# A two-layer graph network on one core: row statistics of both norms from group sums and squared deviations on ScalarE

## The chip, the cores and the metric

The kernel runs on one core of a Trainium2 chip. The metric is the time of one execution on the device in microseconds. A core has five engines with an instruction queue each: TensorE (PE: matrix products, with its weight loads listed apart as PEld), VectorE (DVE), ScalarE (ACT), GpSimd (POOL) and SyncE (SP), which in this kernel issues the transfers (DMA). An engine works through its queue in order; semaphores make it wait for others. So an instruction that waits holds everything behind it in its own queue.

## The reference

128 graphs with 128 nodes of 256 features each go through two layers. Each layer normalises every row, takes the positive part, applies a graph layer and adds the result to its input.

```python
def _layernorm(x, axis=-1, eps=1e-5):
    m = jnp.mean(x, axis=axis, keepdims=True)
    v = jnp.var(x, axis=axis, keepdims=True)
    return (x - m) / jnp.sqrt(v + eps)
...
    h = jnp.maximum(_layernorm(x, axis=-1), 0.0)
    x = x + _L0_gnn_ref(h, adj, L0_gnn_weight, L0_gnn_bias)
    h = jnp.maximum(_layernorm(x, axis=-1), 0.0)
    x = x + _L1_gnn_ref(h, adj, L1_gnn_fc_w, ..., L1_gnn_fp_b)
    return x
```

The first graph layer is `adj @ (h @ weight) + bias`. The second is attention with 8 heads over the graph: logits from one query and one key number per node and head, a mask from the adjacency, a leaky rectifier, a softmax, the weighted sum, a projection back to 256 features, `+ fp_b + h`, and a sigmoid. All is float32.

## The kernel before

**Groups and stages.** The 128 graphs are worked in 32 groups of four (`GB = 4`). A tile of a group has the 128 nodes on the partitions and the four graphs side by side: `xg` is 128 x (4 x 256). A group passes through these stages, and several groups are in work at once, each at another stage:

- `begin` loads x and the adjacency. `n1_stats` takes mean and variance of each row, `n1_apply` (L330) makes h on ScalarE with `Relu(rstd * x + nb)`, where `nb = -mean * rstd`. `first_a` and `first_b` are the products of the first layer (L378, L394); the addition at L401 makes `x1`.
- `n2_stats` and `n2_apply` are the same for `x1`, and give `h2`. `move_h2` (L437) and `turn_h2_blocks` (L441) turn h2 by 16 transfers and a 32 x 32 block transpose; `make_qk` (L464), `turn_qk` (L478 to L484) and `load_k` (L489) make the attention's query and key numbers.
- `masked` (L509, L517, VectorE), `leaky` (L530, ScalarE), `head_max` (L538, VectorE), `exps` (L546, ScalarE, which also sums) and `normal` (L554 on VectorE, L555 on GpSimd) make the attention of one graph each; `move` (L566) and `turn` (L574) turn it.
- Four units a group (`aggregate` L596, `take` L613 to L622, `multiply` L641, `combine` L657 to L676) are the weighted sum and the projection. They use seven products in place of eight, with sums and differences f2 to f6 of the aggregates: `take` copies an aggregate on ScalarE (f0 L613, f3 L615, f1 L621) or works on VectorE (f4 L617, f6 L618), and GpSimd makes f5 (L619) and f2 (L622). A unit's products run one unit after its aggregates.
- `residual_a` (L680), `residual_b`, `sigmoid`, `finish` (L695), `store`.

**Row statistics.** `stats` works on half a group: for each of two graphs a `bn_stats` (L296) over 256 elements and a `bn_aggr` (L297) that gives mean and variance, all on VectorE. `rdev` adds epsilon on VectorE (L308) and raises to the power -0.5 on GpSimd (L312); `shift` forms nb on VectorE (L319). In the loop `rdev_both` and `shift_both` do this together for the second norm of one group and the first norm of the next.

**Order.** All queues follow an order written by hand. A group of the loop has 44 slots; in each slot one step of TensorE's own list is put out (`ORDER`: four aggregates and seven products, four times over), and then the entries of `PLAN` for that slot, in their order in the list. An entry is (slot, which group or "u" for a unit, function, arguments); group 2 means the group two ahead of the current one. The first group has a list of its own, `FIRST_PLAN`, with most of its attention still made by other entries. Ahead of the loop the first groups' early stages are written out one by one; there `scale(..., root=True)` takes a square root on ScalarE (L306) in place of the power.

In the loop before the change, per group: both `n1_stats` at slot 28 (for the group four ahead), `n2_stats` at slots 37 and 40 (three ahead) each behind its `first_b`, `rdev_both` at slot 41, `take` of f1 and f2 at slot 42, `residual_a` at slot 43. In the next group's pass the same norms are then those of "group 2": slot 0 has a `take`, two `masked` and a `leaky`, slot 2 `shift_both`, slot 3 a `take`, the two `n2_apply` and `move_h2`, slots 4 and 5 further attention steps, slot 6 the first half of a `combine`, slot 18 `turn_h2_blocks`, slot 24 `make_qk`, slot 25 `n1_apply`.

Of the kernel before, what the change touches and what calls it, by code (L numbers as in the profile page):

```python
# [9 lines left out]
FP = mybir.dt.float32  # L10
AF = mybir.ActivationFunctionType
ALU = mybir.AluOpType
AX = mybir.AxisListType
PSUM = bass.MemoryType.PSUM

P = 128
D = 256
# [3 lines left out]
GB = 4  # L21
# [3 lines left out]
EPS = 1e-5  # L25
# [3 lines left out]
def gnn_then_gat_kernel(  # L29
# [16 lines left out]
    nc = tc.nc  # L46
    NG = x.shape[0] // GB

    const = ctx.enter_context(tc.tile_pool(name="const", bufs=1))
# [5 lines left out]
    nc.vector.memset(power, -0.5)  # L55
    eps = const.tile([P, 1], FP, name="eps")
    nc.vector.memset(eps, EPS)

    gp = ctx.enter_context(tc.tile_pool(name="group", bufs=2))
    at = ctx.enter_context(tc.tile_pool(name="attention", bufs=2))  # L60
    small = ctx.enter_context(tc.tile_pool(name="small", bufs=3))
# [228 lines left out]
    def stats(s, key, src, b0):  # L290

        if b0 == 0:
            s[key] = small.tile([P, GB, 2], FP, name="mv", tag="mv")
        st = small.tile([P, 2, 6], FP, name="st", tag="st")
        for b in range(2):
            nc.vector.bn_stats(st[:, b, :], src[:, b0 + b, :])  # L296
            nc.vector.bn_aggr(s[key][:, b0 + b, :], st[:, b, :])  # L297

    def rdev(*norms, root=False):

        n = len(norms)
        rstd = small.tile([P, n, GB], FP, name="rstd", tag="rstd")
        for i, (s, key) in enumerate(norms):
            s[key, "by"] = rstd[:, i]
            if root:
                nc.scalar.activation(rstd[:, i], s[key][:, :, 1], AF.Sqrt, bias=eps)  # L306
            else:
                nc.vector.tensor_scalar(rstd[:, i], s[key][:, :, 1], EPS, None, ALU.add)  # L308
        if root:
            nc.vector.reciprocal(rstd, rstd)  # L310
        else:
            nc.gpsimd.tensor_tensor(rstd, rstd, power[:, 0:n], ALU.pow)  # L312

    def shift(*norms):

        for s, key in norms:
            nb = small.tile([P, GB], FP, name="nb", tag="nb")
            rstd = s[key, "by"]
            nc.vector.scalar_tensor_tensor(  # L319
                nb, s[key][:, :, 0], -1.0, rstd, ALU.mult, ALU.mult  # L320
            )
            s[key, "by"] = (rstd, nb)

    def scale(*norms, root=False):
        rdev(*norms, root=root)
        shift(*norms)
# [10 lines left out]

    def n1_stats(s, half):
        stats(s, "n1", s["xg"], 2 * half)

    def n1_apply(s, half):
        if half == 0:
            s["h"] = gp.tile([P, GB, D], FP, name="h", tag="h", bufs=1)
        for b in range(2 * half, 2 * half + 2):
            apply(s, "n1", b, s["h"][:, b], s["xg"][:, b])
# [69 lines left out]
    def rdev_both(s):  # L415
        rdev(*norms_of(s))

    def shift_both(s):
        shift(*norms_of(s))
# [279 lines left out]
    def store(s, b0, nb):  # L699
# [9 lines left out]
    PLAN = [  # L709
        (0, "u", take, 0, 0, 0),  # L710
        (0, 1, masked, 0),
        (0, 1, masked, 1),
        (0, 1, leaky, 0),
        (2, 2, shift_both),
        (3, "u", take, 0, 1, 1),
        (3, 2, n2_apply, 0),
        (3, 2, n2_apply, 1),
        (3, 2, move_h2),
# [41 lines left out]
        (28, 1, move, 0, range(8, 16)),  # L760
        (28, 1, normal, 3),
        (28, 3, turn_blocks),
        (28, 4, n1_stats, 0),
        (28, 4, n1_stats, 1),
        (28, -1, sigmoid, 0, GB),
        (29, -1, finish, 0, GB),
        (29, 3, add_b0),
# [11 lines left out]
        (35, 3, first_a, 1),  # L779
        (36, "u", take, 3, 1, 1),  # L780
        (37, 3, first_b, 0),
        (37, 3, n2_stats, 0),
        (37, 3, make_mask),
        (39, "u", take, 3, 1, 0),
        (40, 3, first_b, 1),
        (40, 3, n2_stats, 1),
        (41, 3, rdev_both),
        (42, "u", take, 3, 0, 1),
        (43, 0, residual_a, 1),
    ]  # L790
# [21 lines left out]
        (17, "u", take, 1, 1, 0),  # L812
        (17, 1, leaky, 0),
        (18, 0, turn_by_products, 3),
        (18, 3, n1_stats, 0),
        (18, 3, n1_stats, 1),
        (20, "u", take, 1, 0, 1),
        (20, 1, masked, 1),
        (20, 2, first_a, 0),
# [6 lines left out]
        (23, 2, first_b, 0),  # L826
        (23, 2, first_b, 1),
        (24, 4, begin),
        (24, 2, n2_stats, 0),
        (24, 2, n2_stats, 1),  # L830
        (24, 2, rdev_both),
        (25, "u", take, 2, 1, 1),
        (25, 1, head_max, 1),
        (25, 1, normal, 0),
        (25, 2, shift_both),
        (26, 2, n2_apply, 0),
# [24 lines left out]
        (34, 3, turn_blocks),  # L861
        (36, "u", take, 3, 1, 1),
        (36, 0, setup_wqk_order),
        (36, 4, n1_stats, 0),
        (36, 4, n1_stats, 1),
        (36, 1, head_max, 3),
        (36, 1, normal, 2),
        (37, 3, first_a, 0),
# [2 lines left out]
        (38, 1, turn, 0),  # L871
        (39, "u", take, 3, 1, 0),
        (39, 3, first_b, 0),
        (39, 3, n2_stats, 0),
        (39, 1, turn, 1),
        (39, 1, normal, 3),
        (40, 1, move, 1),
        (41, 3, first_b, 1),
        (41, 3, n2_stats, 1),
        (41, 3, rdev_both),  # L880
        (42, "u", take, 3, 0, 1),
        (42, 3, make_mask),
        (43, 0, residual_a, 1),
# [80 lines left out]
    n2_stats(s1, 1)  # L964
    normal(s0, 0)
    rdev((s1, "n2"), (s2, "n1"))
    setup_weights(3, 0, True)
    setup_weights(3, 1, True)
# [3 lines left out]
    setup_weights(5, 1, True)  # L972
    normal(s0, 1)
    shift((s1, "n2"), (s2, "n1"))
    setup_weights(6, 0, True)
    setup_weights(6, 1, True)
# [22 lines left out]
    for g in range(NG):  # L999
# [4 lines left out]
        for slot in range(4 * len(ORDER)):  # L1004
            n, i = divmod(slot, len(ORDER))
# [58 lines left out]
```

## Time and profile before

| | |
|---|---|
| median of three runs | 1537.14 us (1533.25, 1537.14, 1537.39) |
| the profiled execution | 1530.25 us, of which 1528.5 us are its span |
| mean granted TensorE clock | 0.997 |
| transfers | 139.18 MB, the 16 DMA engines busy 40% |

The page of the profile gives the busy time of each engine, then the instructions grouped by line (busy time in all, mean duration in ns, idle time of the engine just ahead of them and what ended it). The rows of the statistics on it are these:

```profile
L296 DVE BATCH_NORM_STATS2 st<-x 128x6 f32<-128x256 f32 x128 | 52.5, 410 | 2.0
L312 POOL TENSOR_TENSOR rstd<-rstd,power 128x8 f32<-128x8 f32 (+1 forms) x31 | 50.5, 1629 | 48.0 <-DVE rstd L308 48.0
L296 DVE BATCH_NORM_STATS2 st<-xg 128x6 f32<-128x256 f32 x128 | 50.3, 393 | 3.7 <-DMA xg<-in_x_dram 3.7
L297 DVE BATCH_NORM_AGGREGATE mv<-st 128x2 f32<-128x6 f32 x256 | 46.6, 182 | 8.8
```

The means are durations; instructions of one engine overlap a little, so the pitch from start to start is smaller, and it is the pitch that fills a queue. A timeline line gives start and duration in us, engine, line, operation, tiles, the count, and in square brackets how long the engine had been idle and what released it. A line of the waits gives who waited for whom, then the total in us, how often, and the longest. Busy time by stretch shows the same picture in all groups of the loop; three of them are, with the columns stretch, its length, and busy time (and instructions) of PE, PEld, DVE, ACT and POOL, then TensorE's clock and the transfers:

```profile
562.00:608.00 46.00, 45.87 (x314) 37.34 (x313) 41.43 (x75) 34.84 (x124) 30.03 (x22) 1.00 0.44 97
608.00:653.00 45.00, 44.39 (x300) 35.59 (x299) 39.82 (x67) 33.12 (x117) 28.32 (x22) 1.00 0.43 93
653.00:698.00 45.00, 44.87 (x306) 36.36 (x306) 40.45 (x71) 33.84 (x120) 29.06 (x22) 1.00 0.44 98
```

### The profile page before, as it was taken

The page shows a single profiled execution, that of the slowest core. Times are in us where ns is not written, and L with a number is a line of the kernel's source. Part 1 is how long each engine was busy: PE and PEld are TensorE (multiplying, and loading weights), DVE is VectorE, ACT ScalarE, POOL GpSimd, SP SyncE. Part 2 cuts the span into 40 slices and gives each one's busy share as a digit, 9 for nine tenths or more (in the row PEclk, how much of TensorE's full clock was granted, in tenths as well). Part 3 has the DMA queues.
Part 4 walks back from the last instruction along what each step waited for, and adds up shares of the span by engine and source line. Part 5 has one row for each costly group of instructions (what it writes and reads, how often), then busy time and mean ns, then how long its engine had stood idle before and what let it go on. Part 6 is the DMA issues. An engine that isn't in the chain of part 4 may idle for free.

```text
span 1528.5 us, 30616 instructions
## 1 busy us (share of the span) xinstructions
PE 1481.2 (97%) x9969; PEld 1195.8 (78%) x9969; DVE 1312.9 (86%) x2275; ACT 1101.8 (72%) x3836; POOL 954.4 (62%) x698
## 2 busy tenths in 40 slices
PE   7788999999999999999999999999999999999998
PEld 6577888877788888788887887888778888878776
DVE  5888988888988888998888898888898888898763
ACT  4888677787677788677778776678766778876651
POOL 5556566665566766566766556666556676656563
PEclk9999999999999999999999999999999999999999
DMA  6123344444444444434444434444443444433320
GB/s 188 30 49 79 81 104 107 87 100 96 94 87 105 94 100 94 96 83 104 106 87 98 96 91 92 107 87 99 95 98 84 105 93 101 95 76 81 73 70 28
DMA packets 253736, 139.18 MB, mean 91 GB/s; under 512 B 169972, under 2 KB 221576, under 8 KB 253320
## 3 DMA queue, kind: packets, MB, share of 16 engines
q1 hardware_dynamic: 253576, 137.23, 40.0%
q8 instruction: 78, 1.28, 0.4%
q14 instruction: 82, 0.67, 0.2%
HBM read 39.60 MB, written 17.30 MB: 37 GB/s over the span
## 4 chain that ended last, share of the span: by engine, by line
ACT 32%; DVE 30%; SPq 11%; PE 9%; issue 6%; DMA 6%; POOL 4%; DVEq 0%; ACTq 0%; POOLq 0%
ACT attn L546 13%; ACT attn L530 11%; SPq L566 8%; DVE attn L517 7%; PE acc L641 5%; DVE attn L509 5%; ACT h L330 4%; DVE st L296 3%; DMA attnB<-attn 3%; DVE attnT L574 3%; PE g_ps L596 3%; SPq L437 2%; POOL attn L555 2%; DVE f L617 2%; DVE x L401 2%
## 5 line engine op out<-in xcount | busy, mean ns | idle before, releaser
L641 PEld LDWEIGHTS acc<-wts,f 128*128 128x128 f32 x7168 | 886.8, 192 | 249.3 <-issue 179.5
L641 PE MATMUL acc<-wts,f 128*128 128x128 f32 x7168 | 894.4, 275 | 5.5 <-DVE z L657 5.0
L596 PE MATMUL g_ps<-attnT,h 128*128 128x512 f32 x1024 | 526.5, 597 | 0.0
L546 ACT ACTIVATE attn<-attn,nmax 128x128 f32<-128x128 f32 x1024 | 397.7, 399 | 0.9 <-DVE nmax L538 0.9
L619 POOL TENSOR_TENSOR f<-f,f 128x512 f32<-128x512 f32 x128 | 163.4, 1277 | 341.5 <-DVE f L617 341.0
L530 ACT ACTIVATE attn<-attn,q 128x128 f32<-128x128 f32 x1024 | 313.3, 393 | 34.9 <-DMA attnB<-attn 19.2
L555 POOL TENSOR_TENSOR attn<-attn,total 128x1024 f32<-128x1024 f32 x128 | 246.2, 1923 | 101.6 <-DVE total L554 87.7
L621 ACT COPY f<-g_ps 128x512 f32<-128x512 f32 x128 | 73.9, 577 | 260.0 <-PE g_ps L596 260.0
L622 POOL TENSOR_TENSOR f<-f,f 128x512 f32<-128x512 f32 x128 | 208.8, 1632 | 9.6 <-ACT f L621 6.9
L546 ACT ACTIVATION_READ_ACCUMULATOR attn<-attn,nmax 128x1 f32 x1024 | 202.5, 198 | 0.0
L517 DVE TENSOR_TENSOR attn<-attn,mask 128x1024 f32<-128x1024 f32 x128 | 190.3, 1487 | 4.5
L538 DVE TENSOR_REDUCE nmax<-attn 128x8 f32<-128x1024 f32 x128 | 153.9, 1202 | 18.8 <-ACT attn L530 18.6
L596 PEld LDWEIGHTS g_ps<-attnT,h 128*128 128x128 f32 x1024 | 155.7, 192 | 8.0 <-issue 7.1
L509 DVE STREAM_TRANSPOSE attn<-kq 128x1024 f32<-128x1024 f32 x128 | 157.0, 1226 | 5.5 <-DMA kq<-k_mem 5.4
L574 DVE STREAM_TRANSPOSE attnT<-attnB 128x1024 f32<-128x1024 f32 x124 | 148.5, 1216 | 8.6 <-DMA attnB<-attn 5.9
L617 DVE TENSOR_TENSOR f<-g_ps,f 128x512 f32<-128x512 f32 x128 | 87.0, 680 | 48.0 <-issue 26.3
L394 PE MATMUL x_ps<-w_sb,ahT 128*128 128x256 f32 x512 | 121.3, 381 | 1.4 <-ACT ahT L385 1.4
L685 POOL TENSOR_TENSOR z<-z,h 128x256 f32<-128x256 f32 x128 | 90.7, 731 | 39.9 <-DVE z L657 39.9
L613 ACT COPY f<-g_ps 128x512 f32<-128x512 f32 x128 | 74.5, 582 | 41.6 <-PE g_ps L596 41.6
L394 PEld LDWEIGHTS x_ps<-w_sb,ahT 128*128 128x128 f32 x512 | 93.1, 191 | 12.4 <-ACT ahT L385 2.2
L695 DVE SCALAR_TENSOR_TENSOR z<-z,x 128x1024 f32<-128x1024 f32 (+1 forms) x33 | 89.2, 2703 | 7.9 <-ACT z L691 7.9
L618 DVE TENSOR_TENSOR f<-f,g_ps 128x512 f32<-128x512 f32 x128 | 86.4, 675 | 0.0
(100 smaller groups left out, 1286.1 us busy)
## 6 DMA issues: line engine op xcount, KB each, us to landing
attnB<-attn SPq DMA_DIRECT2D x992, 64.0 KB, 2.0
xg<-in_x_dram SPq DMA_DIRECT2D x32, 512.0 KB, 4.1
out_dram<-z SPq DMA_DIRECT2D x31, 512.0 KB, 3.1
h2B<-h SPq DMA_DIRECT2D x464, 32.0 KB, 1.9
ag<-in_adj_dram SPq DMA_DIRECT2D x32, 256.0 KB, 4.6
agB<-in_adj_dram SPq DMA_DIRECT2D x116, 64.0 KB, 4.4
fcw<-in_L_gnn_fc_w_dram SPq DMA_DIRECT2D x2, 1024.0 KB, 6.9
fpw<-in_L_gnn_fp_w_dram SPq DMA_DIRECT2D x1, 2048.0 KB, 14.1
```

The costliest lines, as they stand in the source:

```text
L394: nc.tensor.matmul(op[:, bb, :], lhsT=s["ahT"][:, 2 * b2 + bb, c, :], rhs=w0_sb[:, c, :], start=(c == 0), stop=(c == NC - 1),)
L509: nc.vector.transpose(s["v", b], s["kq"][:, :, b].unsqueeze(3).to_broadcast([P, NB, H, Q]),)
L517: nc.vector.tensor_tensor(a, a, s["mask"][:, b, :] .rearrange("p (j c) -> p j c", c=Q) .unsqueeze(2) .to_broadcast([P, NB, H, Q]), ALU.add,)
L530: nc.scalar.activation(a[:, :, h, :], a[:, :, h, :], AF.Prelu, bias=s["q"][:, b, h : h + 1], alpha=0.01,)
L538: nc.vector.tensor_reduce(nmax, a.rearrange("p j h c -> p h j c"), AX.XY, ALU.max, negate=True)
L546: nc.scalar.activation(a[:, :, h, :], a[:, :, h, :], AF.Exp, bias=s["nmax", b][:, h : h + 1], accum_out=s["total", b][:, h : h + 1],)
L555: nc.gpsimd.tensor_tensor(a, a, total.unsqueeze(1).unsqueeze(3).to_broadcast([P, NB, H, Q]), ALU.mult)
L574: nc.vector.transpose(aT.rearrange("p h (i r) -> p i h r", r=Q), s["ab", b // 2][:, :, b % 2])
L596: nc.tensor.matmul(u["g", b, c], lhsT=s["h2"][:, 2 * pair + b].rearrange("p j c q -> p (j c q)")[:, ts(c, P)], rhs=s["aT", 2 * pair + b][: ...
L619: nc.gpsimd.tensor_tensor(new(5), f[4], f[0], ALU.subtract)
L622: nc.gpsimd.tensor_tensor(new(2), f[1], f[5], ALU.subtract)
L641: nc.tensor.matmul(acc[:, slot, :], lhsT=u["f"][m][:, h, :], rhs=wt[m][:, half * HU + h, :], start=(half == 0 and h == 0 and m in FIRST), ...
```

## The change

Two new functions stand beside `stats`. `sums` takes one negated sum per row over all graphs given (four for n1, two for n2) with a single `tensor_reduce` on VectorE. `squares` runs one `Square` activation per graph on ScalarE, of `256 * x - sum`, whose accumulated output is 256 cubed times the variance; what it writes itself goes to a tile that nobody reads. `rdev` multiplies by the inverse of that factor in the instruction that adds epsilon, and `shift` takes the sum, divided by 256, in place of the mean.

```diff
+    def sums(s, key, src, b0, nb):
+        if b0 == 0:
+            s[key, "sum"] = small.tile([P, GB], FP, name="nsum", tag="nsum", bufs=4)
+            s[key, "sq"] = small.tile([P, GB], FP, name="sq", tag="sq", bufs=4)
+        nc.vector.tensor_reduce(
+            s[key, "sum"][:, b0 : b0 + nb], src[:, b0 : b0 + nb], AX.X, ALU.add, negate=True
+        )
+
+    def squares(s, key, src, b0, nb):
+        for b in range(b0, b0 + nb):
+            nc.scalar.activation(
+                squared, src[:, b], AF.Square, bias=s[key, "sum"][:, b : b + 1], scale=float(D),
+                accum_out=s[key, "sq"][:, b : b + 1],
+            )
...
-                nc.vector.tensor_scalar(rstd[:, i], s[key][:, :, 1], EPS, None, ALU.add)
+                if (key, "sq") in s:
+                    var, by = s[key, "sq"], float(D) ** -3
+                else:
+                    var, by = s[key][:, :, 1], 1.0
+                nc.vector.tensor_scalar(rstd[:, i], var, by, EPS, ALU.mult, ALU.add)
...
     PLAN = [
         (0, "u", take, 0, 0, 0),
         (0, 1, masked, 0),
+        (0, 2, rdev_both),
         (0, 1, masked, 1),
         (0, 1, leaky, 0),
-        (2, 2, shift_both),
         (3, "u", take, 0, 1, 1),
+        (3, 2, shift_both),
         (3, 2, n2_apply, 0),
...
-        (28, 4, n1_stats, 0),
-        (28, 4, n1_stats, 1),
+        (28, 4, n1_sums),
...
         (37, 3, first_b, 0),
-        (37, 3, n2_stats, 0),
+        (37, 3, n2_sums, 0),
+        (37, 4, n1_squares),
+        (37, 3, n2_squares, 0),
         (37, 3, make_mask),
         (39, "u", take, 3, 1, 0),
         (40, 3, first_b, 1),
-        (40, 3, n2_stats, 1),
-        (41, 3, rdev_both),
+        (40, 3, n2_sums, 1),
+        (40, 3, n2_squares, 1),
         (42, "u", take, 3, 0, 1),
```

`FIRST_PLAN` is changed in the same way: the n1 sums at slots 18 and 36, their squares at 20 and 39; for the group two ahead the n2 sums at slot 24, the squares and `rdev_both` at slot 25 (behind a `take` and a `head_max`); for the one three ahead the n2 sums and squares at slots 39 and 41, with `rdev_both` left to slot 0 of the next group. The statistics written out ahead of the loop still use `stats`.

More of the change, by code (lines that the diff above doesn't have):

```diff
@@ L57, in gnn_then_gat_kernel @@
     nc.vector.memset(eps, EPS)
+    squared = const.tile([P, D], FP, name="squared")
     gp = ctx.enter_context(tc.tile_pool(name="group", bufs=2))
@@ L318, in shift @@
             rstd = s[key, "by"]
-            nc.vector.scalar_tensor_tensor(
-                nb, s[key][:, :, 0], -1.0, rstd, ALU.mult, ALU.mult
-            )
+            if (key, "sum") in s:
+                mean, by = s[key, "sum"], 1.0 / D
+            else:
+                mean, by = s[key][:, :, 0], -1.0
+            nc.vector.scalar_tensor_tensor(nb, mean, by, rstd, ALU.mult, ALU.mult)
             s[key, "by"] = (rstd, nb)
@@ L339, in n1_stats, with n1_sums, n1_squares, n2_sums @@
         stats(s, "n1", s["xg"], 2 * half)
+    def n1_sums(s):
+        sums(s, "n1", s["xg"], 0, GB)
+    def n1_squares(s):
+        squares(s, "n1", s["xg"], 0, GB)
+    def n2_sums(s, half):
+        sums(s, "n2", s["x1"], 2 * half, 2)
+    def n2_squares(s, half):
+        squares(s, "n2", s["x1"], 2 * half, 2)
     def n1_apply(s, half):
@@ L814, in gnn_then_gat_kernel @@
         (18, 0, turn_by_products, 3),
-        (18, 3, n1_stats, 0),
-        (18, 3, n1_stats, 1),
+        (18, 3, n1_sums),
+        (20, 3, n1_squares),
         (20, "u", take, 1, 0, 1),
@@ L828, in gnn_then_gat_kernel @@
         (24, 4, begin),
-        (24, 2, n2_stats, 0),
-        (24, 2, n2_stats, 1),
-        (24, 2, rdev_both),
+        (24, 2, n2_sums, 0),
+        (24, 2, n2_sums, 1),
+        (25, 2, n2_squares, 0),
+        (25, 2, n2_squares, 1),
         (25, "u", take, 2, 1, 1),
         (25, 1, head_max, 1),
+        (25, 2, rdev_both),
         (25, 1, normal, 0),
@@ L863, in gnn_then_gat_kernel @@
         (36, 0, setup_wqk_order),
-        (36, 4, n1_stats, 0),
-        (36, 4, n1_stats, 1),
+        (36, 4, n1_sums),
         (36, 1, head_max, 3),
@@ L873, in gnn_then_gat_kernel @@
         (39, 3, first_b, 0),
-        (39, 3, n2_stats, 0),
+        (39, 3, n2_sums, 0),
+        (39, 4, n1_squares),
+        (39, 3, n2_squares, 0),
         (39, 1, turn, 1),
@@ L878, in gnn_then_gat_kernel @@
         (41, 3, first_b, 1),
-        (41, 3, n2_stats, 1),
-        (41, 3, rdev_both),
+        (41, 3, n2_sums, 1),
+        (41, 3, n2_squares, 1),
         (42, "u", take, 3, 0, 1),
```

## The prediction

> **What bounds the kernel now.** I read the page's first two parts, the waits, and then the timelines of all engines over one ordinary group of four graphs (606 to 655 us).
>
> ```profile
> span 1528.5 us, 30616 instructions
> PE 1481.2 (97%) x9969; PEld 1195.8 (78%) x9969; DVE 1312.9 (86%) x2275; ACT 1101.8 (72%) x3836; POOL 954.4 (62%) x698
> PE qk_ps L464 <- DVE h2T L441: 8.0, 19, 2.8
> PE acc L641 <- DVE z L657: 5.0, 6, 2.7
> ```
>
> TensorE is 97% busy, and where it waits inside the loop, it waits for VectorE: for h2T (L441) or for a combined accumulator (L657). The L464 instructions of the loop start at 147.6 us for the first and at 1417.1 for the last of its 29 times, 28 periods apart: with 0.4 us off, since the last start is the last of its own 16, 45.3 us a group. What would TensorE need unhindered? From start to start in its timeline a product of L641 (8 matmuls) takes 0.89 us, an aggregation of L596 0.86; a group has 28 and 16 of them, 25.0 + 13.8, and L378 1.79, L394 twice 1.73, L464 0.59, L478 0.11 make 44.75. So **the whole prize in the loop is 28 x 0.55 = 15 us**, however much VectorE work goes.
>
> The 0.55 consists of the hold before L464 in every group (0.20 is shown as idle; by starts, with modelled ends left aside, the 16 matmuls ahead begin at 643.60 and fill 1.78, to 645.38, so it is 0.35) and of a hold at L641 in some:
>
> ```profile
> 633.84 2.02 PE L641 MATMUL acc<-wts,f 128*128 128x128 f32 x16 [0.42 <-DVE z L657]
> 645.75 0.67 PE L464 MATMUL qk_ps<-h2T,wqk 128*32 128x128 f32 x16 [0.20 <-DVE h2T L441]
> ```
>
> Both have the same cause. VectorE's timeline shows no idle time between the turn at 615.84 and the head maxima at 646.46: a queue of 30 us, with the statistics of x1 in its first third. ScalarE is the second half of the circle: it starts at the first normalisation (629.26), works without a break to 659 us, and the f3 copies of that stretch release the turned k, the transfers behind it and so the next 615.84. So time saved in VectorE ahead of 629.08 (nb, L319) shortens the circle, and nothing else does.
>
> **The change part by part.** From the page's groups of instructions:
>
> ```profile
> L538 DVE TENSOR_REDUCE nmax<-attn 128x8 f32<-128x1024 f32 x128 | 153.9, 1202 | 18.8 <-ACT attn L530 18.6
> L330 ACT ACTIVATE h<-x,nb,rstd 128x256 f32<-128x256 f32 x128 | 66.4, 590 | 23.3 <-DVE nb L319 23.3
> ```
>
> and, from the timelines of ScalarE, VectorE and GpSimd over that group:
>
> ```profile
> 622.08 0.59 ACT L621 COPY f<-g_ps 128x512 f32<-128x512 f32 x1 [8.21 <-PE g_ps L596]
> 618.14 0.65 DVE L401 TENSOR_TENSOR x<-x_ps,xg 128x512 f32<-128x512 f32 x1
> 618.82 0.43 DVE L296 BATCH_NORM_STATS2 st<-x 128x6 f32<-128x256 f32 x1
> ...
> 621.09 0.68 DVE L401 TENSOR_TENSOR x<-x_ps,xg 128x512 f32<-128x512 f32 x1
> ...
> 623.34 1.65 POOL L312 TENSOR_TENSOR rstd<-rstd,power 128x8 f32<-128x8 f32 x1 [1.39 <-DVE rstd L308]
> 624.95 1.89 POOL L622 TENSOR_TENSOR f<-f,f 128x512 f32<-128x512 f32 x1
> 626.79 1.27 POOL L680 TENSOR_TENSOR h<-h,fpb_j 128x512 f32<-128x512 f32 x1
> 629.08 0.22 DVE L319 SCALAR_TENSOR_TENSOR nb<-mv,rstd 128x4 f32<-128x4 f32 x2
> ```
>
> *Input sums (n1), slot 28.* Removed: four pairs of L296 and L297, 0.53 us a pair from start to start, 2.1 us. Added: one reduction of 128x1024, the size of L538, 1.2 us. Saved 0.9 us, but off the path: the turn at 615.84 waits for a DMA (0.64 us idle), so VectorE only idles longer there. Worth 0.
>
> *x1 sums (n2), slots 37 and 40.* Removed twice two pairs, 1.1 us each (618.82 to 619.91). Added twice a reduction of 128x512; the trace has none over whole rows, so between half of L538 (0.60) and all of it (1.20); I take 0.65, since L538's time runs with its elements. Saved 0.45 each, 0.9 on the path (between 0 and 1).
>
> Here a rule speaks against the change. The Trainium skill, "VectorE: DVE Perf Modes", section Rules for kernel authors, calls `tensor_reduce` the slowest operation of this engine and says to restructure around it. Taken as it stands, no step to more reductions should gain. But L538 makes 1024 elements in 1.20 us and the eight bn instructions need 2.1 for the same, so the rows decide: 0.9 gained where the rule would put 0 or less.
>
> *Squares on ScalarE.* Eight a group, 128x256. Four of L330 start to end take 2.08 us, a pitch of 0.50; reading out the accumulator adds 0.09 (exps of L546 follow each other at 0.385, leaky units of the same size at 0.29). So 0.59 each, 4.7 us a group, 139 us for the 236 of them (n1 of 29 groups, n2 of 30); upper bound 0.80, if each waits for the full 0.20 us of the accumulator's row. The skill, "ScalarE: Activation LUTs", sections What ACT_TABLE_LOAD costs and Rules for kernel authors, would give 0.09 less (one pointer operand in place of two), and it leaves multiplications to VectorE. By that rule n2 alone would need products (half of L517's 1.23 us, twice) and two more reductions there, 2.5 us for 0.9 saved: 1.6 us a group lost on the path, 45 us in all. But the rows show VectorE without a gap here and ScalarE with one, so the engine that is slower by the element is the cheaper: I keep 0.59 and the idle time. What hides them: ScalarE is idle before 622.08 for 8.21 us. The four n1 squares run there from 613.9 to 616.3, and the first n2 pair at 619.5 to 620.7. Cover is enough even at 0.80. Only the second n2 pair is exposed: it waits for the second sum. Should Square need another table set, the one load of the trace (1283 ns) would come twice a group; the trace shows Prelu, Exp, Tanh, Relu and copies under one set, and I give the other 3 in 100.
>
> *rdev moved from slot 41 to behind the first mask, shift from slot 2 to 3.* Neither issues a DMA; SP's transfers of h2 (L437) wait for the h behind nb and move with it. VectorE doesn't wait for the squares at once: it has a mask to do first (2.4 us). But GpSimd gets the power (L312) behind L622 and L680 instead of ahead of them, and L622 waits for an f1 copy that on ScalarE now stands behind the second pair of squares. So there is a **new wait**: nb for the power. Queued behind nb on VectorE are the head maximum, two masks, the combination and h2T; all of the circle. The f1 copy itself, at 623.8 for 622.7, holds nobody: its product starts at 626.2, that of f2 (L622) at 631.5.
>
> The two ways to nb, from the second L401. It starts at 620.6 instead of 621.09 (0.45 saved before it) and ends at 621.25.
> - Through VectorE: sum 0.65, mask 2.4, rdev 0.2, mask 2.4, and up to 1.0 because an addition of L517 takes 2.26 instead of 1.23 us beside L680 (now at 626.89, and again likely): 626.9 to 627.9.
> - Through ScalarE and GpSimd: sum 0.7, two squares 1.25, copy 0.6, L622 1.3 to 1.9, L680 1.25, power 1.65, hand-over 0.1: 628.1 to 628.7; with squares at 0.80 and all collisions up to 629.2.
>
> The second ends last. So nb comes at 628.1 to 629.2, I take 628.5, **0.6 us earlier** than 629.08. The first mask needs kq, whose last transfer is issued about 619.6 and lands in 1.7 us, 621.3; it would start at 621.95, so this is covered, by 0.6. 0.6 is more than the 0.35 before L464 and enough for most of the holds at L641. What is late next is TensorE itself, at 44.75. I take 44.85 to 44.9, since single holds (1.3 us at 917 us) have other causes: **28 x 0.43 = 12 us saved**.
>
> *The first two groups lose.* In group 0 the reductions and squares stand on the way to the first turned h: ScalarE ends its exps at 91.45 and squares four times (2.4 us, with the last read-out to 94.0), so rdev comes at 94.0 instead of 92.42: 1.6 us, and TensorE's hold of 3.06 us at 96.97 grows by it. At the start of group 1 the power stands behind f1's copy, L622, the mask (L355) and L680 as well: sums of the same rows put nb at 129.7 instead of 127.83, 1.9 us, and the hold of 2.83 us before L464 grows. Together **3.5 us lost**. The statistics written out ahead of the loop stay as they are.
>
> Sum: -12 + 3.5 = -8.5 us. The profiled execution took 1530.25 us (1528.5 of span and 1.75 around it), so 1521.75, a factor of 0.9944. The median of the runs shown is 1537.14, 7 us above that execution; the factor gives **1528.6 us**.
>
> **Rivals.**
> 1. *No net gain (22 in 100).* The power ends at the late end, 629.1: nb stands where it was, the loop keeps 45.3, the 3.5 us remain: 1540.6. For it: the chain's many members. Against: it needs the upper value of each.
> 2. *Slower: nb waits for the power (22 in 100).* The place is slot 3, the point from which it decides is a power that ends after 629.0. TensorE has no slack to VectorE (holds of 0.35 already), so every 0.1 us later costs 28 x 0.1 = 2.8 us. At 0.5 us late, 14 + 3.5 = 17.5: 1554.7. For it: L622 took 2.25 us once in this group beside a VectorE operation, and GpSimd now does L622 and L680 beside both masks. Against: 0.6 us of room by the rows.
> 3. *The full prize (8 in 100).* Every hold in the loop goes and the start-up loses little: -15, 1522.
> 4. *Table switches (3 in 100).* Two loads a group; the first falls in idle time, the second ahead of the leaky units at 625.74, which would have been ready 1.4 us earlier: the gain goes, 1541.
> 5. The forecast: 45 in 100, with an own range of 1522 to 1535.
>
> A difference under 0.3% (4.6 us) can't be told from none here. Faster: nine tenths of the forecast and rival 3, 0.49. Same: the rest of the forecast, most of rival 1, 0.21. Slower: rivals 2 and 4 and what is left of rival 1, 0.30. The range leaves out the best of rival 3 and the worse half of rival 2: 1518 to 1554.
>
> **What would show it.** In the changed profile: VectorE's busy time near 1250 us (2.2 us a group less by the rows), ScalarE's up by about 140, no second kind of ACT_TABLE_LOAD in the loop; L464 no longer waiting for L441, at a period of 44.8 to 44.9; a wait of nb for the power that was not there before; the f1 copy about 1 us later with nobody held. The step is wrong if nb comes later against the first L394 of its group than the 15.1 us of now (613.97 to 629.08), if the squares' pitch is over 0.8, or if the period stays at 45.3. The prediction fails if the start-up costs over 8 us or the circle is closed by something that I took as covered, kq's landing above all.

## The result, and the profile after

The changed kernel takes 1526.01 us (median of six runs, 1523.49 to 1528.84), the kernel before 1537.16 beside it: **0.9933 of the time, with a 95% interval of 0.9914 to 0.9953**. The forecast was 0.9944. The profiled executions are 1524.06 and 1530.25 us, only 6.2 us apart, because the one of before was faster than every one of its own runs here; its granted clock was 0.997, that of after's profile 0.994, and the last section comes back to that.

Lines that the change moved down: the apply L330 is now L355, nb L319 is L346, `rdev` L308 is L331, the power L312 is L335; L401 is L438, L441 is L478, L464 is L501, L517 is L554, L621 and L622 are L658 and L659, L641 is L678, L657 is L694, L680 is L717. The sums are L307, the squares L313. First the head of the page after, with its chain of work that ended last:

```profile
span 1522.3 us, 30708 instructions
PE 1480.8 (97%) x9969; PEld 1199.4 (79%) x9969; DVE 1264.9 (83%) x1892; ACT 1239.1 (81%) x4308; POOL 944.2 (62%) x698
PE 58%; DVE 10%; ACT 10%; POOL 7%; SPq 6%; issue 3%; DMA 3%; DVEq 0%; POOLq 0%; ACTq 0%
```

VectorE has lost 48 us of work and ScalarE has gained 137, and it is the third line that shows what this did: before, the chain was 32% ScalarE, 30% VectorE and 9% TensorE. The circle through VectorE and ScalarE is no longer what ends last; TensorE is. The waits say the same:

```profile
PE acc L678 <- DVE z L694: 4.7, 2, 2.8
PE qk_ps L501 <- DVE h2T L478: 2.2, 4, 1.1
DVE nb L346 <- POOL rstd L335: 13.6, 30, 1.7
```

TensorE's wait for h2T came 19 times and now comes 4 times. The third line is the wait that the prediction announced: in 30 of its pairs nb stands still for the power, 0.45 us each. The groups of instructions that bear on the sum:

```profile
L307 DVE TENSOR_REDUCE nsum<-x 128x2 f32<-128x512 f32 x60 | 41.0, 685 | 2.0
L331 DVE TENSOR_SCALAR rstd<-sq 128x4 f32<-128x4 f32 x59 | 38.2, 690 | 1.5 <-ACT squared L313 1.5
L554 DVE TENSOR_TENSOR attn<-attn,mask 128x1024 f32<-128x1024 f32 x128 | 161.4, 1261 | 4.5
L313 ACT ACTIVATE squared<-x,nsum 128x256 f32<-128x256 f32 x120 | 61.3, 511 | 125.9 <-DVE nsum L307 123.9
```

The reduction of 128x512 is 0.69 us (0.65 taken). L331 is the surprise: 0.69 us on average for four numbers per row, where the same instruction took 0.17 before. The mask additions fell from 1487 to 1261 ns. Both come from one place, which the timeline shows in the group that the prediction read (start, duration, engine, line):

```profile
618.60 0.65 DVE L438 TENSOR_TENSOR x<-x_ps,xg 128x512 f32<-128x512 f32 x1
...
622.58 0.51 ACT L313 ACTIVATE squared<-x,nsum 128x256 f32<-128x256 f32 x1 [1.27 <-DVE nsum L307]
...
624.43 1.59 POOL L659 TENSOR_TENSOR f<-f,f 128x512 f32<-128x512 f32 x1 [2.50 <-ACT f L658]
...
624.81 1.31 DVE L331 TENSOR_SCALAR rstd<-sq 128x4 f32<-128x4 f32 x2
...
625.99 1.27 POOL L717 TENSOR_TENSOR h<-h,fpb_j 128x512 f32<-128x512 f32 x1
...
626.04 1.23 DVE L546 STREAM_TRANSPOSE attn<-kq 128x1024 f32<-128x1024 f32 x1
...
627.21 1.65 POOL L335 TENSOR_TENSOR rstd<-rstd,power 128x8 f32<-128x8 f32 x1
627.31 1.23 DVE L554 TENSOR_TENSOR attn<-attn,mask 128x1024 f32<-128x1024 f32 x1
...
628.90 0.23 DVE L346 SCALAR_TENSOR_TENSOR nb<-nsum,rstd 128x4 f32<-128x4 f32 x2 [0.37 <-POOL rstd L335]
```

The small L331 is issued while GpSimd is in L659 and lasts until that has ended: 1.31 us for 0.24. That pushes the second mask addition past GpSimd's L717, so it takes 1.23 where it took 2.26. One collision has gone and another has come, of the same size. From the first addition of x1 to nb the group takes 628.90 - 618.60 = 10.30 us; before it was 629.08 - 618.14 = 10.94. VectorE was ready for nb after 9.94 us, 1.00 earlier than before, and 0.36 of that goes in waiting for the power. The gain in this group is 0.64 us (0.6 forecast).

Where the 6.2 us between the two profiles are: in the loop from L501 to L501 the 28 periods have a mean of 45.01 us for 45.33, -8.8 us; the first L501 of the loop comes at 151.0 for 147.6, +3.4; behind the last one 111.0 for 111.8, -0.8. In this loop the granted clock is 1.00 in both profiles, so its -8.8 us owes nothing to the clock; the +3.4 ahead of it does.

### The profile page after: what moved, and what is told of

Same layout as the page of the kernel before. It is cut to its first block, busy times and chain, and to the rows that moved or that the text cites. A ratio compares the mean times of both kernels' runs of the same rounds, so it can differ in the third digit from the quotient of the medians.

```text
span 1522.3 us, 30708 instructions
## 1 busy us (share of the span) xinstructions
PE 1480.8 (97%) x9969; PEld 1199.4 (79%) x9969; DVE 1264.9 (83%) x1892; ACT 1239.1 (81%) x4308; POOL 944.2 (62%) x698
## 3 DMA queue, kind: packets, MB, share of 16 engines
q8 instruction: 78, 1.28, 0.4%
## 4 chain that ended last, share of the span: by engine, by line
PE 58%; DVE 10%; ACT 10%; POOL 7%; SPq 6%; issue 3%; DMA 3%; DVEq 0%; POOLq 0%; ACTq 0%
PE acc L678 32%; PE g_ps L633 18%; PE x_ps L431 5%; ACT attn L583 3%; SPq L474 3%; ACT attn L567 3%; PE ah_ps L415 3%; SPq L603 3%; POOL f L659 2%; ACT h L355 2%; POOL rstd L335 2%; POOL h L717 1%; POOL attn L592 1%; DVE attnT L611 1%; DVE attn L546 1%
## 5 line engine op out<-in xcount | busy, mean ns | idle before, releaser
L678 PEld LDWEIGHTS acc<-wts,f 128*128 128x128 f32 x7168 | 889.1, 192 | 246.1 <-issue 185.7
L678 PE MATMUL acc<-wts,f 128*128 128x128 f32 x7168 | 894.8, 275 | 4.9 <-DVE z L694 4.7
L656 POOL TENSOR_TENSOR f<-f,f 128x512 f32<-128x512 f32 x128 | 163.2, 1275 | 307.2 <-DVE f L654 306.5
L659 POOL TENSOR_TENSOR f<-f,f 128x512 f32<-128x512 f32 x128 | 201.5, 1574 | 92.0 <-ACT f L658 89.5
L554 DVE TENSOR_TENSOR attn<-attn,mask 128x1024 f32<-128x1024 f32 x128 | 161.4, 1261 | 4.5
L313 ACT ACTIVATE squared<-x,nsum 128x256 f32<-128x256 f32 x120 | 61.3, 511 | 125.9 <-DVE nsum L307 123.9
L546 DVE STREAM_TRANSPOSE attn<-kq 128x1024 f32<-128x1024 f32 x128 | 156.6, 1224 | 4.9 <-DMA kq<-k_mem 4.9
L611 DVE STREAM_TRANSPOSE attnT<-attnB 128x1024 f32<-128x1024 f32 x124 | 148.5, 1216 | 10.3 <-DMA attnB<-attn 7.7
L355 ACT ACTIVATE h<-x,nb,rstd 128x256 f32<-128x256 f32 x128 | 66.8, 592 | 39.0 <-DVE nb L346 39.0
L658 ACT COPY f<-g_ps 128x512 f32<-128x512 f32 x128 | 73.3, 573 | 27.4 <-PE g_ps L633 27.2
```

The source lines that it names most:

```text
L546: nc.vector.transpose(s["v", b], s["kq"][:, :, b].unsqueeze(3).to_broadcast([P, NB, H, Q]),)
L554: nc.vector.tensor_tensor(a, a, s["mask"][:, b, :] .rearrange("p (j c) -> p j c", c=Q) .unsqueeze(2) .to_broadcast([P, NB, H, Q]), ALU.add,)
L611: nc.vector.transpose(aT.rearrange("p h (i r) -> p i h r", r=Q), s["ab", b // 2][:, :, b % 2])
L656: nc.gpsimd.tensor_tensor(new(5), f[4], f[0], ALU.subtract)
L659: nc.gpsimd.tensor_tensor(new(2), f[1], f[5], ALU.subtract)
L678: nc.tensor.matmul(acc[:, slot, :], lhsT=u["f"][m][:, h, :], rhs=wt[m][:, half * HU + h, :], start=(half == 0 and h == 0 and m in FIRST), ...
```

## Experiments

The theory: the cheaper sums shorten VectorE's queue ahead of nb, the squares are hidden on ScalarE, and the new order is needed so that VectorE doesn't stand still for them. Rivals: the order alone does it; the first norm's statistics do it; nothing but less VectorE work counts; a collision has gone by luck. The table has every run. The start of h2 is that of the first normalisation of x1, behind the first product of L394 in its group (median over the loop); the last column is the mean of the second mask addition over the last 29 groups. The time before is the median on the same chip; the ratio on record is not the quotient of the two medians beside it and differs from it by up to 0.0023.

| run | ratio, 95% interval | us (before) | period, median / mean | h2 starts | 2nd mask addition |
|---|---|---|---|---|---|
| before | | | 45.15 / 45.33 | 14.58 | 2.18 |
| after | 0.9933, 0.9914 to 0.9953 | 1526.0 (1537.2) | 44.89 / 45.01 | 14.32 | 1.23 |
| a_n1_only | 1.0001, 0.9981 to 1.0020 | 1534.3 (1533.9) | 45.12 / 45.31 | 14.57 | 2.18 |
| b_n2_only | 0.9944, 0.9926 to 0.9962 | 1525.8 (1533.9) | 44.89 / 44.98 | 14.32 | 1.23 |
| c_order_only | 1.0042, 1.0027 to 1.0057 | 1540.1 (1533.9) | 45.45 / 45.54 | 14.92 | 1.23 |
| d_old_order | 1.0125, 1.0100 to 1.0150 | 1552.8 (1533.9) | 45.84 / 45.97 | 15.31 | 2.18 |
| g_n1_sq_twice | 0.9927, 0.9893 to 0.9961 | 1525.6 (1535.8) | 44.89 / 45.06 | 14.32 | 1.23 |
| h_n2_sq_twice | 1.0273, 1.0240 to 1.0307 | 1581.2 (1535.8) | 46.78 / 46.84 | 16.24 | 1.50 |
| f_residual_later | 1.0044, 1.0030 to 1.0057 | 1543.4 (1535.8) | 45.47 / 45.57 | 14.94 | 1.26 |
| l_residual_slot7 | 1.0015, 1.0002 to 1.0028 | 1538.9 (1536.3) | 45.36 / 45.37 | 13.87 | 1.23 |
| k_squares_vector | 1.0236, 1.0207 to 1.0266 | 1569.1 (1536.3) | 46.21 / 46.54 | 15.74 | 1.23 |
| i_no_stats | 0.9872, 0.9849 to 0.9895 | 1514.9 (1536.3) | 44.89 / 44.89 | | 2.22 |
| e2_first_before | 0.9899, 0.9874 to 0.9923 | 1522.7 (1535.8) | 44.89 / 45.00 | 14.32 | 1.23 |
| m_combined | 1.0009, 0.9996 to 1.0022 | 1536.7 (1536.3) | 45.36 / 45.46 | 13.87 | 1.23 |

**One norm alone.** *a* is the kernel before with only n1 by sums and squares; *b* is the kernel after with n1 by bn statistics again.

```diff
 a
-        (28, 4, n1_stats, 0),
-        (28, 4, n1_stats, 1),
+        (28, 4, n1_sums),
...
+        (37, 4, n1_squares),
 b
-        (28, 4, n1_sums),
+        (28, 4, n1_stats, 0),
+        (28, 4, n1_stats, 1),
...
-        (37, 4, n1_squares),
```

> The kernel before with only the input's statistics (n1) from sums and squares; x1's stay on bn_stats, rdev and shift in their old places. Theories S and O: worth nothing, period 45.3, time within 3 us of before, although VectorE is 30 us less busy. If every us of VectorE counts, the period falls by up to 0.4 us and the time by 9 us.

> The changed kernel with the input's statistics (n1) back on bn_stats and bn_aggr, so that only x1's come from sums and squares; order as changed. Both theories: the loop doesn't miss the n1 sums, since VectorE waits for a transfer behind them: period 45.0, time as with the whole change within 3 us, VectorE's busy time 30 us higher, ScalarE's 75 us lower. If every us of VectorE counts, the period rises by up to 0.9 us to 45.3 or more.

a is where before is, b where after is, in time, period and start of h2. All of it is in the second norm. VectorE's busy time falls by 24 us in a's profile (1289.1 for 1312.9) and buys nothing: the less work lies ahead of a turn that waits for a transfer.

**The order alone, and the sums without it.** *c* is the kernel before with only the move, *d* the kernel after without it.

```diff
 c (the reverse in d)
         (0, 1, masked, 0),
+        (0, 2, rdev_both),
         (0, 1, masked, 1),
         (0, 1, leaky, 0),
-        (2, 2, shift_both),
         (3, "u", take, 0, 1, 1),
+        (3, 2, shift_both),
...
-        (41, 3, rdev_both),
```

> The kernel before with only the order changed: rdev behind the first mask and shift one step later, in the loop and in the first group; the statistics stay bn_stats and bn_aggr on VectorE. Theory S (the gain of the loop is the 0.9 us that the sums of x1 take off VectorE's queue): nothing is taken off, nb stays at 14.4 us behind the first product of L394, the period stays at 45.3 us, the time within 3 us of before. Theory O (the gain is the collision of the second mask addition with residual_a on GpSimd, 2.26 against 1.23 us, that the order removes): the addition takes 1.23 us, nb comes at 13.4 to 14.1, the period falls to 44.9 to 45.0, and the time falls by 9 us or more, as with the whole change.

> The changed kernel with rdev back at slot 41 and shift back at slot 2 in the loop. Theory S: the sums still save 0.9 us, but VectorE now waits some 1.4 us for the last squares before the masks, so nb comes at 14.2 to 14.9 behind the first product of the layer and about half of the gain or all of it goes: period 45.0 to 45.4. Theory O: the power runs ahead of residual_a again, the second mask addition is back at 2.26 us, nb at 14.9 or later, period 45.3 or more, the time at or above that of before.

Each alone makes the kernel slower. The timeline of c, in the same stretch as above:

```profile
629.80 1.34 DVE L517 TENSOR_TENSOR attn<-attn,mask 128x1024 f32<-128x1024 f32 x1
...
630.02 2.25 POOL L680 TENSOR_TENSOR h<-h,fpb_j 128x512 f32<-128x512 f32 x1
631.07 1.30 DVE L308 TENSOR_SCALAR rstd<-mv 128x4 f32<-128x4 f32 x2
...
633.55 1.23 DVE L517 TENSOR_TENSOR attn<-attn,mask 128x1024 f32<-128x1024 f32 x1
```

The collision of the mask addition has gone (1.03 us less) and that of L308 has come (1.06 us more), here with L680, which is itself stretched from 1.27 to 2.25 us. From L401 to nb it is 11.00 us, nothing saved. So the freed addition is no gain of its own. That c is even slower than before has its cause in the first mask addition, which now starts during L622 (median 1.62 us for 1.23 in 25 groups; 1.34 in the one shown): nb comes at 14.73 us behind the first product for 14.40. In d the waits show the other half:

```profile
DVE rstd L331 <- ACT squared L313: 41.0, 30, 1.5
...
PE acc L678 <- DVE z L694: 17.1, 30, 2.2
```

With `rdev` in its old slot VectorE stands still 1.37 us in each of 30 groups for the second pair of squares, with the masks queued behind, and TensorE pays for it at L678. d's figures (mask addition 2.18, nb at 15.13 us, slower than before) are also those that theory O forecast, so d alone doesn't decide between the two; c does, where the addition is freed and nothing is gained. Between after and d the two collisions nearly cancel (1.03 us more for the mask addition, 1.07 less for L331), and the 1.00 us by which nb is later is about the 1.37 of standing still less the wait for the power, which has gone.

**Squares twice.** *g* repeats the n1 squares, *h* the second pair of the n2 squares: one line doubled each.

```diff
 g
         (37, 4, n1_squares),
+        (37, 4, n1_squares),
 h
         (40, 3, n2_squares, 1),
+        (40, 3, n2_squares, 1),
```

> The changed kernel with the input's squares made twice over in the loop (four more activations a group, 2.6 us). They stand in ScalarE's idle time, 3.18 us before the first square of x1. Theory S: hidden, nb at 14.13, period 45.0, 0.993 of before within 0.002, with ScalarE's busy time 75 us higher. Rival (a fuller ScalarE as such, or its memory traffic, slows other engines): period 45.2 or more.

> The changed kernel with the second pair of x1's squares made twice over in the loop (two more activations a group, 1.28 us at the pitch of 0.64 us in the changed kernel's trace). Theory S with the wait for the power as the end of the path: everything behind these squares on ScalarE and GpSimd moves by 1.28 us, nb comes at 15.4 us instead of 14.13 behind the first product, and by the line through the kernels so far (45.09 at 14.40, 45.45 at 14.73, 45.84 at 15.13) the period is 46.1 and the time 34 us above the changed kernel, about 1.5% above before. Rival R (ScalarE hides its squares wholly, and what VectorE no longer does is all that counts): no change against the changed kernel, 0.993 of before.

Four more squares of n1 a group, 61 us more of ScalarE (1300.0), cost nothing. Two more behind the second sum make the group 1.9 us longer. They delay `rdev`, the f1 copy, L659 and L717 by 1.28 us, and L717 then runs into a mask addition (2.25 us for 1.27), so nb comes 1.92 later: the period of 46.78 us lies above the 46.1 expected, which had left this collision out. The waits for nb in h:

```profile
DVE nb L346 <- POOL rstd L335: 80.7, 31, 2.8
```

80.7 us for 13.6: nb is tied to the power, and through it to the second pair of squares. Over before, c, d, h and after, the period follows the start of h2 one to one: 14.58, 14.92, 15.31, 16.24 give 45.15, 45.45, 45.84, 46.78; at 14.32 it is 44.89.

**L717 out of the way.** If nb waits for a power behind L659 and L717, a later L717 should free 1.27 us. *f* puts it behind nb, *l* further on.

```diff
-        (43, 0, residual_a, 1),
 f
         (3, 2, shift_both),
+        (3, -1, residual_a, 1),
 l
         (7, "u", take, 0, 1, 0),
+        (7, -1, residual_a, 1),
```

> The changed kernel with residual_a of the second pair on GpSimd behind the power instead of ahead of it (next group, after shift). The power then starts 1.2 us earlier, so nb waits for VectorE alone and comes at 13.7 to 13.8 us, unless the second mask addition collides again. Theory F (TensorE at 44.89 us a group is the bound once nb comes by 14.1): the period stays at 44.9 to 45.0 and the time within 3 us of the changed kernel. Theory S without a floor: 0.35 us a group, 10 us more gained, 0.987 of before.

> The changed kernel with residual_a of the second pair on GpSimd at slot 7 of the next group, behind f5. The power starts 1.2 us earlier and nothing stands beside nb, so h2 starts at 13.8 to 14.0 us behind the first product instead of 14.32. By the line that the runs so far give (44.89 at 14.32, 45.45 at 14.92, 46.78 at 16.24: one us for each us) a period of 44.4 to 44.6 would follow: rival, no floor, 0.985 of before. Theory F (TensorE's own work is 44.89 us): the period stays at 44.89, with fewer longer ones, time within 3 us of the changed kernel, 0.991 to 0.993 of before.

Both are slower than after, which none of the expectations had. In f, nb itself now meets L717:

```profile
678.21 1.84 POOL L717 TENSOR_TENSOR h<-h,fpb_j 128x512 f32<-128x512 f32 x1
678.84 1.30 DVE L346 SCALAR_TENSOR_TENSOR nb<-nsum,rstd 128x4 f32<-128x4 f32 x2
```

In l h2 does start 0.45 us earlier (13.87), as meant. But L717 now stands ahead of L659 in GpSimd's queue, and L659 starts just before the second of the combination's two instructions at L694, which lasts until L659 has ended: the two take 1.73 us in place of 0.93, and h2T stands behind them in the queue:

```profile
637.63 1.27 POOL L717 TENSOR_TENSOR h<-h,fpb_j 128x512 f32<-128x512 f32 x1
...
638.74 1.73 DVE L694 TENSOR_TENSOR z<-w,v 128x256 f32<-128x256 f32 x2
...
638.86 1.45 POOL L659 TENSOR_TENSOR f<-f,f 128x512 f32<-128x512 f32 x1
...
648.73 0.67 PE L501 MATMUL qk_ps<-h2T,wqk 128*32 128x128 f32 x16 [0.39 <-DVE h2T L478]
```

So l is the case in which the start of h2 does not tell the period, because the loss lies behind it. Of the three places tried for L717, the one it had is the best.

**Squares on VectorE.** *k* is b with the second norm's squares as one product and one more reduction on VectorE, of the rows without their mean taken off.

```diff
-        squares(s, "n2", s["x1"], 2 * half, 2)
+        bs = ts(half, 2)
+        nc.vector.tensor_tensor(squared, s["x1"][:, bs], s["x1"][:, bs], ALU.mult)
+        nc.vector.tensor_reduce(s["n2", "sq"][:, bs], squared, AX.X, ALU.add)
```

> x1's squares on VectorE (a product of 128x512 and a reduction of it for each half, without taking the mean off first), n1 on bn statistics, order as changed; nothing of the statistics is on ScalarE. It is what the rule would do that leaves elementwise work to VectorE. Theory: 2.4 us more in VectorE's queue on the path, of which 0.37 fill its wait for the power: h2 starts at 16.2 to 16.6, period 46.7 to 47.1, 1.025 to 1.035 of before. Rival (ScalarE's squares are as much on the path as VectorE's would be): no slower than the changed kernel by more than 1%.

0.0236 of 1536 us are 36 us above before, where the prediction had worked out 45 for this way (1.6 us a group; the mean period rose by 1.2), and ratio, period and start of h2 lie below the ranges expected here. The direction was right and the size too large; why, no run shows. Against b, the same with the squares on ScalarE, the difference is 0.0292 or 45 us. Here the rule of the Trainium skill that the prediction cites ("ScalarE: Activation LUTs", Rules for kernel authors: multiplications to VectorE) loses to the question which engine has a gap.

**No statistics in the loop's lists.** *i* drops the sums, squares, `rdev` and `shift` from both lists and applies a fixed factor and shift in their place.

```diff
-        rstd, nb = s[key, "by"]
+        rstd, nb = s.get((key, "by"), (fixed[:, 0], fixed[:, 1]))
```

> The changed kernel with no row statistics at all in the loop: the normalisations from the third group's n1 or n2 on use a fixed factor of 1 and a shift of 0, and sums, squares, rdev and shift of those are left out. Theory F: period 44.89 and no less, since TensorE's work is the same; the start-up gains 2 to 5 us; 0.985 to 0.992 of before. Rival (no floor): nb isn't waited for at all, the circle is 2 us or more shorter, the period 43 or less, the time 3% or more below before.

All 28 periods are 44.89 us. That is TensorE's own floor, and after's median period is the same: in more than half of its groups the statistics cost nothing any more. What i has over after (0.9872 for 0.9933, some 9 us) cannot be the ordinary period: 28 x 0.12 = 3.4 us are single longer groups, such as 46.10 at 916 us, and its first product of the turned h2 in the loop (L504 there) comes at 147.9 for 151.0, 3.1 us. The other 3 us are about what the clock made: the granted clock of i's four executions is 0.994 on average, that of after's six 0.992, and by the last section 0.001 of it goes with 1.2 to 1.5 us.

**The first groups as before.** *e2* takes the change in the loop only; the first list has bn statistics again, with `rdev_both` of its last slots left to the next group. *m* is e2 with l's move.

```diff
 e2
-        (24, 2, n2_sums, 0),
-        (24, 2, n2_sums, 1),
-        (25, 2, n2_squares, 0),
-        (25, 2, n2_squares, 1),
+        (24, 2, n2_stats, 0),
+        (24, 2, n2_stats, 1),
+        (24, 2, rdev_both),
...
-        (25, 2, rdev_both),
```

> The changed kernel with the first group's list as it was before (bn statistics there, rdev right behind those of x1), and the new order from the second group on. Theory: the start-up loses 1.6 us to the squares ahead of the first turned h, so TensorE's hold at 95 us falls from 4.7 back to 3.1 us; the loop stays at 45.0; time 1 to 4 us below the changed kernel, 0.991 to 0.993 of before. Rival (what the changed profile loses in its first 150 us is TensorE's half-clock stretches, not the list): no gain, the first L464 of the loop at 151 us again.

> The first group's list as before the change (as in the run with that alone), and in the loop residual_a of the second pair on GpSimd at slot 7, behind f5, where it stands neither ahead of the power nor beside nb. The first h2 then starts at 13.8 to 14.0 us behind the first product, 0.4 us before TensorE can miss it. Theory (the list of the first group was 1.6 us or more lost, TensorE is the bound at 44.89 us): start-up as in the run with the old list, period 44.89 in nearly every group, 0.987 to 0.990 of before. Rival (no floor): period 44.5, 0.980 of before.

TensorE's hold in group 0, in the waits, first of after, then of e2:

```profile
PE h2T_ps L489 <- ACT h L355: 7.6, 2, 4.7
```

```profile
PE h2T_ps L489 <- ACT h L355: 5.9, 2, 3.1
```

The 1.7 us of this hold are given back (the first L501 of the loop comes at 150.3 for 151.0, with one more stretch at half clock than after), and 0.9899 is the best ratio of those that compute the same. It beats before; against after the intervals overlap a little (0.9874 to 0.9923 and 0.9914 to 0.9953), and the two didn't run in one comparison, so its lead isn't settled: 5 us by the ratios, 3.3 by the medians (1522.7 and 1526.0), 0.9 by the profiled executions (1523.12 and 1524.06). m loses it all to l's collision.

## Why the prediction held, step by step

- *n1 worth 0, all squares but the second n2 pair hidden:* a and b confirm the first, g the hidden squares of n1 and h the exposed pair; the first n2 pair was not tested by itself.
- *The way through ScalarE and GpSimd ends last, nb 0.6 us earlier:* it does (0.37 us idle for the power, h), and 0.64 was measured in the group read. The squares' pitch is 0.64 us (622.58 to 623.22) where 0.59 was taken, the reductions 0.69 for 0.65. In the square itself the page cited in the prediction (the Trainium skill, "ScalarE: Activation LUTs", What ACT_TABLE_LOAD costs) was right: with one pointer operand fewer it is 0.08 us shorter than L355 (511 ns for 592). The read-out behind it was mis-sized: from its start to the next square it takes 0.22 us, where the exps had shown 0.09; why, no run shows. The group read, though, was one of the slowest: nb came 15.1 us behind its first L394 product there, while the median before was 14.40; after it is 14.13. In the median group the gain is 0.27, and the median period fell by the same 0.26.
- *28 x 0.43 = 12 us in the loop:* mis-sized, it was 8.8. The floor by starts was 44.75, and i measures 44.89; of the 0.14, 0.09 is a pause of TensorE ahead of L501 that stays when nobody is waited for. From the old mean to that floor there were 28 x 0.44 = 12.3 us, and 3.4 of them remain as single longer groups.
- *An addition of L517 "takes 2.26 instead of 1.23 us beside L680 (now at 626.89, and again likely)":* **this step failed.** It takes 1.23. The prediction saw the collision of two long instructions and costed `rdev` at 0.2; in fact the short one meets GpSimd and is held 1.07 us, which moves the long one clear. The two errors cancel in nb, as c shows, and that they are of one size is luck. They nearly cancel in the busy time too (L331 has 38.2 us for L308's 7.4, the mask additions 161.4 for 190.3). VectorE's 1264.9 us for "near 1250" have another cause: the 2.2 us a group were taken from durations, but the bn instructions overlap. The prediction's own pitches, twice 0.9 us a group, would have given 1261.
- *3.5 us lost in the first two groups:* 3.4 in the profile, and that they agree is luck. The hold at 97 us grew by 1.67 (1.6 forecast). The second part was put in the wrong place: the hold of 2.83 us before L464 in group 1 went, and those at L678 and behind h grew (1.08 to 2.80, 1.38 to 1.96). Over these holds idle time grew by only some 1.1 us net; the rest is TensorE at half clock, below.
- *One set of tables, ScalarE +140:* no table load in the loop, and +137. The only two loads, at 0.7 and 44.2 us, stand where they stood before (the prediction spoke of one).

The total: by ratio the forecast was 1.7 us too slow. The two profiles show -6.2 us for the -8.5 forecast, the ratio of all runs 0.0067 x 1537 = -10.3; the difference fits the clock, which was 0.003 higher in the profile of before (some 4 us, by the last section). The loop gave less than forecast, and the start-up of this execution cost what was forecast for another reason, so the close total proves none of its terms. Rival 2 had its mechanism right, h shows the wait that it describes, but its point was not reached.

## What to carry to other kernels

Work taken from a busy engine counts only in the stretch where its queue ends last; half of what was taken here was worth nothing, and the other half was worth something only together with an order that keeps that engine from standing still for the engine that now does the work. A short instruction isn't cheap where it is issued while another engine holds what it needs: look at its start, not only at its size. Once the period equals that of the kernel with the stage left out, stop working on that stage and look at the start-up.

## What the runs showed of the hardware

**Some instructions of VectorE and GpSimd shut each other out.** A mask addition, L331, nb or L694's `z<-w,v`, issued while GpSimd is in one of its 128x512 additions, ends with it or after it: 1.31 us for 0.24 (L331), 1.30 for 0.23 (nb in f), 2.26 for 1.23 (mask addition). The other way round GpSimd's 1.27 us became 2.25 (c, h). Others were not held: additions that read an accumulator at L694 kept their 0.42 us, and the turn L546 at 626.04 its 1.23 us beside L717, as in 28 groups of after. Nor does GpSimd's power hold anything: the mask addition at 627.31 starts 0.10 us behind it and takes its 1.23 us, as in 27 groups.

The Trainium skill, "SBUF — State Buffer", section SBUF: two separate sides, describes a pair of ports that goes to whichever starts first for its whole instruction, the other one fully blocked, where VectorE reads two inputs from SBUF or runs in a two-port mode. The rows beside GpSimd's additions agree, held and not held, though no trace tells whether L331 ran in such a mode. The power, also with its inputs in SBUF, does not fit: by the page it would hold the mask addition until 628.86. What had been underrated is that the lock costs a four-element instruction as much as a long one.

**TensorE's clock.** By stretches (length, then busy time of PE, PEld, DVE, ACT, POOL, the granted clock, share and GB/s of transfers), first before, then after, at the same point of the first group:

```profile
76.50:79.90 3.40, 3.40 (x27) 2.88 (x26) 1.98 (x3) 3.40 (x11) 3.32 (x3) 1.00 0.02 5
```

```profile
76.00:79.40 3.40, 3.40 (x12) 2.37 (x12) 0.69 (x1) 3.40 (x10) 3.32 (x3) 0.52 0.02 5
```

TensorE is busy in both. The same eight products of L585 (now L622) and two aggregations take 1.80 us before (76.09 to 77.89) and 3.26 after (75.84 to 79.10), with a hold of 2.9 us ahead of them in both executions. Of such stretches the profile of before has two in its first 160 us, that of after five, each worth up to 1.7 us. The skill, "TensorE: Matmul & The Clock Gate", Part 1, tells of a free-running window of about 3.4 us whose idling halves the rate.

The traces show both the window and why the same hold is punished in one execution and not in another. In each of the 14 profiles the clock changes on a grid of 3.41 us of its own, whose place differs from execution to execution. The hold in question, 2.85 us up to 75.84, falls wholly into one window of after (72.69 to 76.11), and the next window is at half clock; in before an edge at 74.29 splits it into 1.1 and 1.8 us, and nothing follows. Of all windows at full clock in the 14 profiles, each of the 60 in which TensorE stood still for 1.95 us or more (matmul ends are modelled) was followed by one at half clock, none of the 6033 with less than 1.46, and 6 of the 44 between. So the window needn't be idle throughout.

These stretches go with most of the scatter of this kernel on its one core. The 43 executions of before beside i, k, l and m lay between 1530.8 and 1541.8 us; the six with a granted clock of 0.995 to 0.997 took 1530.8 to 1534.1, the three with 0.988 took 1541.4 to 1541.8, and over all of them 0.001 of clock goes with 1.2 us (1.5 in the 35 executions beside a to d). The profile of before, at 1530.25 us and 0.997, was one of the lucky ones.
